# An LSTM with a sign-weight FFN on one core: first x loaded in rows and turned by TensorE, last block's third layer with activations stationary

## The chip, the cores and the metric

One NeuronCore of a Trainium2 chip runs the whole program in one launch. The metric is the device time of one execution in microseconds (us); the median of several runs is compared. The engines are TensorE (PE in the profile, its weight loads PEld), VectorE (DVE), ScalarE (ACT), GpSimd (POOL) and SyncE (SP); SP, ACT and POOL issue DMAs.

## The reference

x is [32, 64, 256], cond is [32, 256]; all floats are float32.

```
xW = einsum('ntd,dg->ntg', x, Wx) + b                # 64 steps, 1024 gate columns
for t in range(64):                                   # LSTM, h0 = cond, c0 = 0
    a = xW[:, t] + h @ Wh
    i, f, o = sigmoid of a's first three quarters;  g = tanh of its last
    c = f * c + i * g;  h = o * tanh(c);  hs[:, t] = h
v = concatenate([hs, -hs], axis=-1)                   # [32, 64, 512]
v = relu(s0 * (v @ pm1(k0))) * 2                      # 1024 features
v = relu(s1 * (v @ pm1(k1))) * 2                      # 1024 features
out = x + s2 * (v @ pm1(k2))                          # 256 features
```

`pm1(k)` is +1 where the boolean is true, else -1. The scales s0, s1, s2 are scalars.

## The kernel before, in words

The 32 batch rows are N, the 64 steps are T. The steps form four blocks of 16 (SB), each block two halves of eight steps. The hidden width of 256 is cut into four quarters of 64 (NQ, HQ); quarter q lies on partitions 32q to 32q+31, so a step's gates fill 128 partitions.

Loading. `load_x` (L88 to L96) brings one half of a block's x with four DMAs, one for each quarter: 32 partitions, eight steps, runs of 64 floats (256 B). `turn_x` (L226 to L231) turns it with VectorE's transpose of 32x32 blocks into `xT`, which holds x with the input dimension on partitions. `load_gates` (L118 to L129) loads column groups ("slots") of Wx or Wh; the gate order in the tile is (3, 0, 1, 2). Wx's rows are taken in two chunks k, since the input dimension 256 is 128 partitions by two. At the start (L132 to L141) SP and ACT issue in this order: x of the first half, Wx's chunks, x of the second half, Wh. GpSimd issues `h_first` (cond, L145), the bias rows and the scales, and then computes the signs and `total`, the product of scales used at the end.

The completion marks of SP's and ACT's DMAs are eight in number and are shared in turn, in the order of issue; a DMA that reuses a mark waits until the earlier DMA has landed.

The start of TensorE (L640 to L643) is two matmuls that fill the gate banks with zeros and eight idle ones (`WARM_UP`), all from a zeroed bf16 tile `idle` of 128x512. Then come the products of x with Wx for the first eight steps: chunk 0, slots 1 and 2, then slots 0 and 3 (L669 to L671, through `x_part` L242); the bias broadcast by matmuls (`copy_bias`, L654); chunk 1 with all slots (L673), each pair of steps evicted by VectorE with the bias added (`evict_x`).

The steps. For each of the 64 steps `gates_from_h` (L301) adds h times Wh to gates that ScalarE has set from the x products, `cell_step` (L319) does the nonlinear part on ScalarE and VectorE, and h is turned into the history. Behind each step's gates TensorE is given a share of other work, by a goal written out by hand: first the remaining x products, then the FFN of the blocks that are complete. FFN operands are split in a high and a low part (fp32r), so each product takes two matmuls.

The last block (`last_block`, L417) has nothing beside it. Its second layer is computed by sums and differences of quarters; its third layer is at L550 to L583. There `layer2` holds a 128x128 piece of `w2` stationary and streams 256 columns of activations; the result has output features on partitions, two banks for each half of the block (eight steps by 32 rows). `turn_out` (L384) turns a result with VectorE into the layout of x, `scale_out` (L387) multiplies by `total` and adds x, and `store` (L377) writes it with four DMAs of 64 KB in runs of 256 B, alternating SP and ACT. The residual x of the block is loaded again by `load_x` at L497.

Of the kernel before, what the change touches and what calls it, by code (L numbers as in the profile page):

```python
# [29 lines left out]
F32 = mybir.dt.float32  # L33
# [3 lines left out]
ALU = mybir.AluOpType  # L37
# [4 lines left out]
def lstm_ffn(ctx: ExitStack, tc: tile.TileContext, x, cond, wx_d, wh_d, b_d, k0_d, k1_d, k2_d, s0_d, s1_d, s2_d, out):  # L42
    nc = tc.nc
    P = 128
    N, T, D = x.shape
    H = cond.shape[1]
    G = 4 * H
    NQ = 4
    HQ = H // NQ
    F0 = k0_d.shape[1]  # L50
    F1 = k1_d.shape[1]
    FC0, FC1 = F0 // P, F1 // P
    SB = 16
    NB = T // SB
    TB = SB * N
    SH = 4
# [5 lines left out]

    FIRST_CHORE = 2
    W2_STEP = 24
    WARM_UP = 8

    SUM_STEP = 28

    const = ctx.enter_context(tc.tile_pool(name="const", bufs=1))
    wpool = ctx.enter_context(tc.tile_pool(name="wx", bufs=1))  # L70
    xpool = ctx.enter_context(tc.tile_pool(name="x", bufs=4))
# [6 lines left out]
    ps_f = ctx.enter_context(tc.tile_pool(name="ps_f", bufs=4, space=PSUM))  # L78
    ps_o = ctx.enter_context(tc.tile_pool(name="ps_o", bufs=2, space=PSUM))
    ctx.enter_context(tc.manual_schedule())  # L80

    def act(shape, dtype, name):
        return apool.tile(shape, dtype, tag="act", name=name)


    xq = {}

    def load_x(i, half, engines, part=slice(0, SB // 2)):  # L88
        if part.start == 0:
            xq[i, half] = xpool.tile([P, SB // 2, HQ], F32, tag="x", name=f"x{i}_{half}")  # L90
        t0 = i * SB + half * (SB // 2)
        for q in range(NQ):
            engines[q % len(engines)].dma_start(
                out=xq[i, half][q * N : (q + 1) * N, part],
                in_=x[:, t0 + part.start : t0 + part.stop, ts(q, HQ)],
            )  # L96
# [5 lines left out]
    wx = wpool.tile([P, 2, G], F32, tag="wx", name="wx")  # L102
    w0 = const.tile([P, 2, F0], F32R, name="w0")
    w1 = const.tile([P, FC0, F1], F32R, name="w1")
    w2 = const.tile([P, 2, FC1, P], F32R, name="w2")

    warm = const.tile([P, 40], F32, name="warm")
    nc.vector.memset(warm, 0.0)
    idle = const.tile([P, 512], mybir.dt.bfloat16, name="idle")
    nc.vector.memset(idle, 0.0)  # L110

    first = warm[:, 4 : 4 + N]
    nc.vector.memset(first[:1], 1.0)
# [4 lines left out]
    def load_gates(t, w_d, slots, engines, chunks=slice(0, 2)):  # L118

        w_rows = w_d.rearrange("(p b) g -> p b g", b=2)  # L120
        s0, n, g0 = slots[0], len(slots), GATES[slots[0]]
        if len(engines) == 1:
            halves = [slice(0, P)]
        else:
            halves = [slice(0, P // 2), slice(P // 2, P)]
        for engine, half in zip(engines, halves):
            engine.dma_start(
                out=t[half, chunks, s0 * H : (s0 + n) * H], in_=w_rows[half, chunks, g0 * H : (g0 + n) * H]
            )  # L129


    both = [nc.sync, nc.scalar]  # L132
    load_x(0, 0, both)
    for k in range(2):
        load_gates(wx, wx_d, (1, 2), [nc.sync], slice(k, k + 1))
        for slot in (0, 3):
            load_gates(wx, wx_d, (slot,), [nc.scalar], slice(k, k + 1))
    load_x(0, 1, both)
    load_gates(wh, wh_d, (1, 2), both)
    load_gates(wh, wh_d, (0,), [nc.scalar])  # L140
    load_gates(wh, wh_d, (3,), [nc.sync])  # L141

    nc.scalar.activation(warm[:, 1:2], warm[:, :1], AF.Sigmoid)
    h_first = const.tile([P, HQ], F32, name="h_first")
    nc.gpsimd.dma_start(out=h_first, in_=cond.rearrange("n (q j) -> q n j", q=NQ))  # L145
    b_rows = b_d.rearrange("(o g h) -> o g h", o=1, g=4)
    nc.gpsimd.dma_start(out=b_row[0][:1, :1], in_=b_rows[:, 3:])
    nc.gpsimd.dma_start(out=b_row[0][:1, 1:], in_=b_rows[:, :1])
    nc.gpsimd.dma_start(out=b_row[1][:1], in_=b_rows[:, 1:3])
    scales = []  # L150
    for i, s_d in enumerate((s0_d, s1_d, s2_d)):
        s = const.tile([P, 1], F32, name=f"s{i}")
# [7 lines left out]
    for i in range(2):  # L160
        t = act([P, 2, F0], U8, f"k0_{i}")
# [17 lines left out]
    total = const.tile([P, 1], F32, name="total")  # L179
# [44 lines left out]
    xT = {}  # L224

    def turn_x(i, half, part=slice(0, SB // 2)):  # L226
        if part.start == 0:
            xT[i, half] = act([P, SB // 2, 2, N], F32, f"xT{i}_{half}")
        nc.vector.transpose(
            xT[i, half][:, part], xq[i, half][:, part].rearrange("p t (j b) -> p t b j", b=2)  # L230
        )  # L231
# [10 lines left out]
    def x_part(p, t, k, slots, start):  # L242

        i, s = divmod(t, SB // 2)
        for q in range(NQ):
            nc.tensor.matmul(  # L246
                p[q * N : (q + 1) * N, t % 2, slots],
                xT[i // 2, i % 2][:, s, k, :],
                wx_q[:, k, q, slots],
                start=start,  # L250
                stop=False,
                skip_group_check=True,
            )
# [123 lines left out]
    def store(b, half, o, engines):  # L377
        t0 = b * SB + half * (SB // 2)
        for q in range(NQ):
            engines[q % len(engines)].dma_start(  # L380
                out=out[:, t0 : t0 + SB // 2, ts(q, HQ)], in_=o[q * N : (q + 1) * N]
            )

    def turn_out(o, p, m):  # L384
        nc.vector.transpose(o[:, :, m, :], p.rearrange("p (t n) -> p t n", n=N))

    def scale_out(o, res):  # L387
        nc.vector.scalar_tensor_tensor(o, o, total, res, ALU.mult, ALU.add)  # L388


    K2, F2, CB = FC0 // 2, F1 // 2, TB // 2
# [25 lines left out]
    def last_block(b):  # L417

        hi, lo = hparts.pop(b)
        full, b11, b2, t, a1 = [], {}, {}, {}, {}  # L420
# [55 lines left out]
        for m in range(FC0):  # L476
            p = ps_f.tile([P, TB], F32, tag="pf", name=f"p0_{b}_{m}")
# [5 lines left out]
            if m < K2:  # L483
# [3 lines left out]
                f = f[:, 0]  # L487
# [6 lines left out]
                    differ(i, m - K2 - 1)  # L494
            yield

        for half in range(2):  # L497
            load_x(b, half, [nc.sync])
        for i in (1, 2):
            differ(i, K2 - 1)  # L500

# [42 lines left out]
        for pair in range(2):  # L544
            product(q, pair, lambda k: sums[4, k], lambda k, n: b2[k][n][:, 1], False, True)
            take(0, 1, pair, q[pair])

        po = [ps_o.tile([P, TB], F32, tag="po", name=f"po{b}_{m}") for m in range(2)]  # L550
        po_half = {
            (0, 0): po[0][:, :CB],
            (0, 1): po[0][:, CB:],
            (1, 0): po[1][:, :CB],
            (1, 1): ps_f.tile([P, TB], F32, tag="pf", name=f"po{b}_2")[:, :CB],
        }

        def layer2(half, m, ks, first, last):
            for k in ks:
                for n in range(2):  # L560
                    nc.tensor.matmul(  # L561
                        po_half[half, m],
                        w2[:, m, k],
                        a1[k, half][n],
                        start=first and k == ks[0] and n == 0 and (half, m) != (0, 1),
                        stop=last and k == ks[-1] and n == 1,
                        skip_group_check=True,
                    )

        os = [act([P, SB // 2, 2, 32], F32, f"o{b}_{half}") for half in range(2)]  # L570
        for ks in (range(K2), range(K2, FC0)):
            for m in range(2):
                layer2(0, m, ks, ks[0] == 0, ks[0] > 0)
        for m in range(2):
            turn_out(os[0], po_half[0, m], m)
        o = os[0].rearrange("p t m j -> p t (m j)")
        scale_out(o, xq[b, 0])
        store(b, 0, o, [nc.sync, nc.scalar])
        for m in range(2):
            layer2(1, m, [*range(K2, FC0), *range(K2)], True, True)  # L580
            turn_out(os[1], po_half[1, m], m)
            scale_out(os[1][:, :, m, :], xq[b, 1][:, :, ts(m, 32)])
        store(b, 1, os[1].rearrange("p t m j -> p t (m j)"), [nc.sync, nc.scalar])  # L583

    def ffn_block(b):
        hi, lo = hparts.pop(b)
# [50 lines left out]
    outputs = deque()  # L637

    p_idle = ps_f.tile([P, TB], F32, tag="pf", name="p_idle")
    for g in gate_banks:  # L640
        nc.tensor.matmul(g, idle[:, :P], idle, start=True, stop=True)  # L641
    for n in range(WARM_UP):
        nc.tensor.matmul(p_idle, idle[:, :P], idle, start=True, stop=True)  # L643
    turn_x(0, 0, slice(0, SB // 4))
    turn_x(0, 0, slice(SB // 4, SB // 2))
    for i in range(4):
        load_bits(i)
    for half in range(2):
# [5 lines left out]
    def copy_bias():  # L654
        p_bias = ps_o.tile([P, 4, HQ], F32, tag="po", name="p_bias")
        for q in range(NQ):
            for i, t in enumerate(b_row):
                nc.tensor.matmul(  # L658
                    p_bias[q * N : (q + 1) * N, 2 * i : 2 * i + 2],
                    first,  # L660
                    t.rearrange("p g (q j) -> p q g j", q=NQ)[:, q],
                    start=(i == 0),
                    stop=True,
                    skip_group_check=True,
                )
        nc.vector.tensor_copy(bias, p_bias)

    banks = [x_bank(t) for t in range(0, SB // 2, 2)]
    for slots in (slice(1, 3), slice(0, 4, 3)):  # L669
        for t in range(SB // 2):  # L670
            x_part(banks[t // 2], t, 0, slots, t % 2 == 0 and slots.start == 1)  # L671
    copy_bias()
    for t in range(SB // 2):  # L673
        x_part(banks[t // 2], t, 1, slice(0, 4), False)
        if t % 2:
            evict_x(banks[t // 2], t - 1)
            if t == 1:
                turn_x(0, 1)
# [89 lines left out]
```

## Time and profile before

| what | value |
|---|---|
| median of 3 runs | 312.65 us (312.47 to 313.43) |
| the profiled execution's own time | 312.31 us |
| its span | 310.5 us |
| mean granted TensorE clock | 0.998 |
| TensorE busy | 304.5 us, 98% of the span |
| VectorE, ScalarE, GpSimd busy | 178.1, 142.0, 6.6 us |

The span is the time from the first to the last event that the profile holds; some 1.8 us lie around it. Busy time counts instructions of an engine, not its waiting for others. The chain of waits is followed back from the last instruction: at each step to what released it. In the list of instructions a line number is that of the kernel, and "x64" means that so many instructions in a row are merged.

### The profile page before, as it was taken

What the parts mean: (1) busy time and instruction counts of PE and PEld (TensorE: products, weight loads), DVE (VectorE), ACT (ScalarE), POOL (GpSimd) and SP (SyncE); (2) the same over time, 40 slices, a digit from 0 to 9 for tenths busy, and PEclk for the clock granted to TensorE, in tenths of its full rate; (3) what the DMA queues carried; (4) which work ended last, traced back from release to release, by engine and by line L of the source; (5) the groups of instructions that cost most, each with busy time, mean ns of one, the idle gap of its engine ahead of it and who ended that gap; (6) DMA issues with size and microseconds to landing.
All of it is one profiled execution on the core that took longest, in us unless ns stands there. A gap on an engine that the chain in (4) does not pass through costs nothing.

```text
span 310.5 us, 9798 instructions
## 1 busy us (share of the span) xinstructions
PE 304.5 (98%) x4138; PEld 242.7 (78%) x4138; DVE 178.1 (57%) x530; ACT 142.0 (46%) x512; POOL 6.6 (2%) x24
## 2 busy tenths in 40 slices
PE   8999999999999999999999999999999999999994
PEld 4888888788777777777777777777777777899993
DVE  2566767777673444355754445567554434698543
ACT  0225566774564543435633434355443333886220
POOL 5300000000000000000000000000000000000000
PEclk9999999999999999999999999999999999999999
DMA  6874001142000000000010000000310000131002
GB/s 192 206 196 99 5 19 38 36 95 65 3 2 0 2 2 0 3 2 0 2 38 22 14 3 0 2 2 13 92 34 2 3 0 2 31 79 27 2 0 69
DMA packets 30587, 10.89 MB, mean 35 GB/s; under 512 B 27720, under 2 KB 29768, under 8 KB 30544
## 3 DMA queue, kind: packets, MB, share of 16 engines
q1 hardware_dynamic: 27136, 8.66, 11.2%
q10 hardware_dynamic: 3168, 1.57, 2.0%
q8 instruction: 32, 0.52, 0.7%
q0 software_dynamic: 240, 0.04, 0.1%
q14 instruction: 11, 0.09, 0.1%
HBM read 8.16 MB, written 2.10 MB: 33 GB/s over the span
## 4 chain that ended last, share of the span: by engine, by line
PE 97%; DVE 1%; ACT 0%; issue 0%; ACTq 0%
PE p L617 30%; PE gates L305 20%; PE px L246 18%; PE p L591 8%; PE po L604 7%; PE gates L452 4%; PE po L561 2%; PE r L452 2%; PE x L452 2%; PE p L479 2%; PE p_idle L643 1%; PE gates L641 0%; DVE a_7l L362 0%; DVE o L388 0%; PE p_bias L658 0%
## 5 line engine op out<-in xcount | busy, mean ns | idle before, releaser
L305 PEld LDWEIGHTS gates<-wh,hist 128*32 128x32 f32 x2016 | 54.6, 109 | 22.3 <-issue 13.4
L305 PE MATMUL gates<-wh,hist 128*32 128x192 f32 x2016 | 68.1, 275 | 0.0
L246 PE MATMUL px<-wx,xT 128*32 128x256 f32 (+1 forms) x1168 | 60.5, 353 | 0.1
L322 ACT ACTIVATE sig<-gates 128x128 f32<-128x128 f32 x64 | 17.7, 277 | 80.6 <-PE gates L305 80.4
L246 PEld LDWEIGHTS px<-wx,xT 128*32 128x32 f32 x1168 | 42.4, 110 | 11.3 <-DVE c_first L652 0.7
L326 DVE TENSOR_TENSOR kept<-sig,c 128x64 f32<-128x64 f32 x63 | 14.2, 225 | 50.0 <-ACT sig L322 49.7
L332 ACT ACTIVATE th<-c 128x64 f32<-128x64 f32 x64 | 16.4, 257 | 31.4 <-DVE c L330 31.4
L334 DVE TENSOR_TENSOR h<-sig,th 128x64 f32<-128x64 f32 x64 | 14.4, 225 | 20.7 <-ACT th L332 20.7
L262 DVE TENSOR_TENSOR xg<-px,bias 128x512 f32<-128x512 f32 x32 | 21.2, 671 | 2.8 <-PE px L246 2.3
L316 ACT COPY gates<-xg 128x192 f32<-128x192 f32 x64 | 20.0, 313 | 1.3 <-DVE xg L262 1.3
L591 PE MATMUL p<-hhi,w 128*128 128x512 f32 x48 | 19.3, 402 | 0.0
L591 PE MATMUL p<-hlo,w 128*128 128x512 f32 x48 | 19.1, 398 | 0.0
L339 DVE STREAM_TRANSPOSE hist<-h 128x64 f32<-128x64 f32 x64 | 15.7, 245 | 2.4
L330 DVE TENSOR_TENSOR c<-kept,new 128x64 f32<-128x64 f32 x64 | 14.4, 224 | 2.2
L324 ACT ACTIVATE sig<-gates 128x64 f32<-128x64 f32 x64 | 14.9, 233 | 0.1
L323 ACT ACTIVATE cand<-gates 128x64 f32<-128x64 f32 x64 | 14.0, 218 | 0.0
L328 DVE TENSOR_TENSOR new<-sig,cand 128x64 f32<-128x64 f32 x64 | 13.9, 217 | 0.0
L317 ACT COPY gates<-xg 128x64 f32<-128x64 f32 x64 | 13.0, 203 | 0.0
L591 PEld LDWEIGHTS p<-hhi,w 128*128 128x128 f32 x48 | 9.0, 188 | 2.2
L591 PEld LDWEIGHTS p<-hlo,w 128*128 128x128 f32 x48 | 9.0, 188 | 2.0
L211 ACT ACTIVATE w<-bits,nsgn,sgn 128x1024 fp32r<-128x1024 uint8 x8 | 9.9, 1241 | 0.0
L617 PE MATMUL p<-a_7h,w 128*128 128x512 f32 x24 | 9.9, 413 | 0.0
(249 smaller groups left out, 602.8 us busy)
## 6 DMA issues: line engine op xcount, KB each, us to landing
x<-in_x_dram SPq DMA_DIRECT2D x60, 64.0 KB, 2.8
out_dram<-o SPq DMA_DIRECT2D x28, 64.0 KB, 1.8
bits<-in_L_ffn_k_dram SPq DMA_DIRECT2D x10, 128.0 KB, 3.2
wx<-in_L_cond_Wx_dram SPq DMA_DIRECT2D x2, 256.0 KB, 4.2
wx<-in_L_cond_Wx_dram ACTq DMA_DIRECT2D x4, 128.0 KB, 4.6
wh<-in_L_cond_Wh_dram ACTq DMA_DIRECT2D x2, 256.0 KB, 5.6
wh<-in_L_cond_Wh_dram SPq DMA_DIRECT2D x2, 256.0 KB, 6.2
k<-in_L_ffn_k_dram SPq DMA_DIRECT2D x2, 256.0 KB, 3.1
```

Of the source, the lines that this page charges most:

```text
L246: nc.tensor.matmul(p[q * N : (q + 1) * N, t % 2, slots], xT[i // 2, i % 2][:, s, k, :], wx_q[:, k, q, slots], start=start, stop=False, ski ...
L262: nc.vector.tensor_tensor(xg[t], p.rearrange("p t g j -> p t (g j)"), b, ALU.add)
L305: nc.tensor.matmul(g[q * N : (q + 1) * N], hT[:, k, :], wh_q[:, k, q, slots], start=False, stop=(k == 1), skip_group_check=True,)
L316: nc.scalar.copy(gates[0], x_t[:, :3])
L322: nc.scalar.activation(sig[:, 0:2, :], gates[0][:, 1:3], AF.Sigmoid)
L324: nc.scalar.activation(sig[:, 2, :], gates[1][:, 0], AF.Sigmoid)
L332: nc.scalar.activation(th, c, AF.Tanh)
L339: nc.vector.transpose(hT, h.rearrange("p (j b) -> p b j", b=2))
L452: nc.tensor.matmul(bank[pair][:, i], a(k)[:, ts(2 * pair + i, P)], b(k, n), start=first and i == 0 and k == 0 and n == 0, stop=last and k ...
L591: nc.tensor.matmul(p, w0[:, k, ts(m, P)], a[:, k, :], start=(n == 0), stop=(n == 3))
L604: nc.tensor.matmul(po[m], w2[:, m, k], a1[k][n], start=(k == 0 and n == 0), stop=(k == FC1 - 1 and n == 1))
L617: nc.tensor.matmul(p1[m], w1[:, k, ts(m, P)], a0[k][n], start=(k == 0 and n == 0), stop=(k == FC0 - 1 and n == 1),)
```

## The change

Four things are changed.

- The first half of block 0 is loaded as rows: a partition is one (step, batch row) pair and holds the 256 inputs, 1 KB. Steps 0 to 3 come in two DMAs (SP and ACT, two steps each), steps 4 to 7 in one (ACT). TensorE turns them against an identity in float32, VectorE copies the result to `xT`. GpSimd makes the identity (a memset and an `affine_select`) ahead of its DMAs, and `h_first` moves behind the bias rows.
- Wx's pieces are issued in another order and cut, and the products follow it: chunk 0 of steps 0 to 3 in both pairs of slots, then steps 4 to 7. The bias matmuls move behind the second step of chunk 1.
- The warm-up is three idle matmuls ahead of the first turn and two behind it (eight before), from a bf16 tile of 128x128 that is read four times over.
- In the last block, the third layer holds 128 columns of activations stationary (four steps by 32 rows) and streams a row of `w2`, 256 columns. The result has (step, batch row) on partitions, so it is scaled and added to x from PSUM in one instruction and stored unturned: two DMAs of 64 KB for each four steps, one on SP and one on ACT, in runs of 1 KB. The residual x is loaded in the same layout, four DMAs of 128 KB on SP.

```diff
-    WARM_UP = 8
+    WARM_UP = (3, 2)
...
+    x_in = x
+    def rows_of(t, t0, n):
+        return t[:, t0 : t0 + n].rearrange("n t d -> t n d")
...
+    idle = const.tile([P, P], mybir.dt.bfloat16, name="idle")
+    nc.vector.memset(idle, 0.0)
     nc.vector.memset(warm, 0.0)
-    idle = const.tile([P, 512], mybir.dt.bfloat16, name="idle")
-    nc.vector.memset(idle, 0.0)
...
+    ident = act([P, P], F32, "ident")
+    nc.gpsimd.memset(ident, 1.0)
+    nc.gpsimd.affine_select(
+        out=ident, in_=ident, pattern=[[-1, P]], compare_op=ALU.is_equal, fill=0.0, base=0, channel_multiplier=1
+    )
     both = [nc.sync, nc.scalar]
-    load_x(0, 0, both)
-    for k in range(2):
-        load_gates(wx, wx_d, (1, 2), [nc.sync], slice(k, k + 1))
-        for slot in (0, 3):
-            load_gates(wx, wx_d, (slot,), [nc.scalar], slice(k, k + 1))
+    x_first = xpool.tile([P, 2, D], F32, tag="x", name="x_first")
+    for s, engine in enumerate(both):
+        engine.dma_start(out=x_first[ts(s, P // 2), 0], in_=rows_of(x_in, s * SH // 2, SH // 2))
+    load_gates(wx, wx_d, (1, 2), both, slice(0, 1))
+    nc.scalar.dma_start(out=x_first[:, 1], in_=rows_of(x_in, SH, SH))
+    load_gates(wx, wx_d, (3,), [nc.sync], slice(0, 1))
+    load_gates(wx, wx_d, (0,), [nc.scalar], slice(0, 1))
+    load_gates(wx, wx_d, (1, 2, 3), [nc.sync], slice(1, 2))
+    load_gates(wx, wx_d, (0,), [nc.scalar], slice(1, 2))
     load_x(0, 1, both)
...
-        for half in range(2):
-            load_x(b, half, [nc.sync])
+        res = [xpool.tile([P, 2, D], F32, tag="x", name=f"res{half}") for half in range(2)]
+        for i in range(NQ):
+            nc.sync.dma_start(out=res[i // 2][:, i % 2], in_=rows_of(x_in, b * SB + i * SH, SH))
...
+        po = [ps_o.tile([P, TB], F32, tag="po", name=f"po{b}_{i}") for i in range(2)]
+        po += [ps_f.tile([P, TB], F32, tag="pf", name=f"po{b}_{2 + i}") for i in range(2)]
+        def layer2(i, ks):
+            half, cols = i // 2, ts(i % 2, P)
             for k in ks:
                 for n in range(2):
                     nc.tensor.matmul(
-                        po_half[half, m],
-                        w2[:, m, k],
-                        a1[k, half][n],
...
+                        po[i][:, :D].rearrange("p (q m j) -> p q m j", q=NQ, m=2),
+                        a1[k, half][n][:, cols],
+                        w2[:, :, k].rearrange("p m (q j) -> p q m j", q=NQ),
+                        start=k == order[half][0] and n == 0,
+                        stop=k == order[half][-1] and n == 1,
                     )
+        def finish(i):
+            o = act([P, D], F32, f"o{b}_{i}")
+            nc.vector.scalar_tensor_tensor(o, po[i][:, :D], total, res[i // 2][:, i % 2], ALU.mult, ALU.add)
+            for s, engine in enumerate((nc.sync, nc.scalar)):
+                t0, n = b * SB + i * SH, SH // 2
+                engine.dma_start(out=rows_of(out, t0 + s * n, n), in_=o[ts(s, P // 2)])
+        order = [[*range(FC0)], [*range(K2, FC0), *range(K2)]]
         for ks in (range(K2), range(K2, FC0)):
-            for m in range(2):
-                layer2(0, m, ks, ks[0] == 0, ks[0] > 0)
...
+            for i in range(2):
+                layer2(i, ks)
+        for i in range(2):
+            finish(i)
+        for i in range(2, 4):
+            layer2(i, order[1])
+            finish(i)
...
+    def turn_first(i):
+        p = ps_o.tile([P, 2, SH, N], F32, tag="po", name=f"px_first{i}")
+        for k in range(2):
+            nc.tensor.transpose(p[:, k].rearrange("p t n -> p (t n)"), x_first[:, i, k::2], ident)
+        for k in range(2):
+            nc.vector.tensor_copy(xT[0, 0][:, ts(i, SH), k, :], p[:, k])
...
-    for n in range(WARM_UP):
-        nc.tensor.matmul(p_idle, idle[:, :P], idle, start=True, stop=True)
-    turn_x(0, 0, slice(0, SB // 4))
-    turn_x(0, 0, slice(SB // 4, SB // 2))
+        nc.tensor.matmul(g, idle, zeros, start=True, stop=True)
+    warm_up(WARM_UP[0])
+    turn_first(0)
+    warm_up(WARM_UP[1])
...
-    for slots in (slice(1, 3), slice(0, 4, 3)):
-        for t in range(SB // 2):
-            x_part(banks[t // 2], t, 0, slots, t % 2 == 0 and slots.start == 1)
-    copy_bias()
+    for i in range(2):
+        for slots in (slice(1, 3), slice(0, 4, 3)):
+            for t in range(i * SH, (i + 1) * SH):
+                x_part(banks[t // 2], t, 0, slots, t % 2 == 0 and slots.start == 1)
+            if i == 0 and slots.start == 1:
+                turn_first(1)
     for t in range(SB // 2):
         x_part(banks[t // 2], t, 1, slice(0, 4), False)
+        if t == 1:
+            copy_bias()
```

## The prediction

> **What bounds the kernel now.** I read the page first, for the engine that fills the span and for the chain that ends last.
>
> ```profile
> span 310.5 us, 9798 instructions
> PE 304.5 (98%) x4138; PEld 242.7 (78%) x4138; DVE 178.1 (57%) x530; ACT 142.0 (46%) x512; POOL 6.6 (2%) x24
> PE 97%; DVE 1%; ACT 0%; issue 0%; ACTq 0%
> ```
>
> TensorE works 304.5 of 310.5 us. What it does not fill is about 1.2 us before its first instruction and 4.5 us after its last, so an edit counts only if it moves TensorE's first useful product, lengthens TensorE's stream, or moves what follows the last matmul. A shift at the start passes to the end nearly one to one. Next the chain of waits at both ends (start, duration, what):
>
> ```profile
> 2.27 3.23 PE p_idle L643 x8
> 5.51 1.89 PE px L246 x64
> ...
> 298.26 7.69 PE po L561 x64
> 305.95 0.02 issue
> 305.98 0.46 DVE o L385
> 306.43 0.03 issue
> 306.46 0.48 DVE o L388
> ```
>
> Useful products begin at 5.51, when the idle warm-up matmuls end; x was ready just before (the timeline has the two turns of x on VectorE from 4.32 for 0.77, to 5.09). After the last matmul come a turn, a scaling and a store: 306.94 to 310.5. The DMA view of 306.9 to 309.2 shows the last store's bytes from 307.76 to 309.08, so 0.8 us from result to first byte, 1.3 us of bytes, 1.45 us from last byte to the end of the span.
>
> Then what a DMA engine moves, from the windows table (length, five engines' busy time, clock, DMA share of 16 engines, GB/s):
>
> ```profile
> 18.00:19.00 1.00, 1.00 (x25) 0.85 (x21) 0.64 (x4) 0.55 (x4) 0.00 (x0) 1.00 1.02 352
> 308.50:309.00 0.50, 0.00 (x0) 0.00 (x0) 0.00 (x0) 0.00 (x0) 0.00 (x0) 0.98 1.08 245
> ```
>
> Loads of 2 and 1 KB rows: 352 / 1.02 / 16 = 21.6 GB/s per engine. Stores of 256 B rows: 245 / 1.08 / 16 = 14.2 GB/s per engine.
>
> Last, how transfers are spread. Every transfer of SP and ACT in before has 32 or more steps as the outermost count of both sides. The change makes transfers whose DRAM side is (t, n, d) with t outermost: 2 steps for the first x pieces and all eight last stores, 4 for the second x piece and the residual loads. One transfer of before resembles them: `h_first` (L145), 4 outermost steps in DRAM against 128 partitions, issued by GpSimd.
>
> ```profile
> DMA packets 30587, 10.89 MB, mean 35 GB/s; under 512 B 27720, under 2 KB 29768, under 8 KB 30544
> ```
>
> Between 2 and 8 KB lie 30544 - 29768 = 776 packets. The 2 KB rows of Wx (256), Wh (256) and k0 (256) make 768; the other 8 are `h_first`, 32 KB in packets of 4,096 B, each 16 rows of 256 B. Sixteen engines would have had 8 rows each, 2,048 B. So at most eight engines carried it: a transfer with few outermost steps was not spread over all. That row decides my forecast.
>
> **The change, part by part.**
>
> *Third layer.* 64 matmuls of 128x256 before and after, with 64 loads of 128 columns, 0.12 us apart. Only which operand stands still is exchanged, and 256 columns stream either way: no change. A tile of four steps is now complete as rows, and the first ends with the 24th matmul: 298.10 + 23 x 0.12 + 0.28 = 301.1.
>
> *Tail on VectorE.* The turn (0.46 + 0.03) goes. Each tile takes one scaling of 256 columns, 0.48 by L388. The first tile is ready at 301.7, the last at 306.46 instead of 306.94.
>
> *Stores.* Bytes start 0.8 us after a tile, at 302.5. In all 524,288 B leave. On two engines that is 262,144 B each, at 21.6 GB/s 12.1 us. The tiles come 0.9 to 2 us apart and each needs 3.0 us, so there is no gap: 302.5 + 12.1 + 1.45 = 316.1, **5.5 us later** than 310.5. Bounds with two engines: 25 GB/s, the fastest 0.1 us slice of the opening (401 GB/s over 16), gives 10.5 us and +3.9; 14.2 GB/s gives 18.5 us and +11.9. I take 21.6, because the new rows are 1 KB. On sixteen engines the last 131,072 B take 0.6 us: 306.46 + 0.8 + 0.6 + 1.45 = 309.3, 1.2 us earlier.
>
> The Trainium skill (DMA: Bandwidth & Descriptors, "Why a DMA increments its semaphore by 16 and not by 1") says that a transfer uses the largest number of engines up to 16 that divides the outermost count of both sides, the lowest-numbered ones. `h_first` agrees, on another queue and without giving the exact number; by the rule the tail is +5.5, by the spread of before's own stores it is -1.2.
>
> *First x.* SP and ACT issue at 0.73 as before, first bytes at 1.7. On two engines 65,536 B each at 21.6 GB/s take 3.0 us; with about 0.5 for the completion mark x stands at 5.2, where 16 engines give about 2.9. TensorE now needs two f32 transposes and a copy of 128 columns on VectorE. Neither has a row: a transpose lies between 0.12 (a 256-column matmul here) and 0.43 (a slow warm-up), I take 0.3; the copy lies between 0.23 (64 columns) and 0.42 (256), I take 0.3. Two warm-ups of 0.43 stand behind the transposes in TensorE's order: 5.2 + 0.6 + 0.86 gives 6.7, by VectorE alone 6.1; 6.4, **+1.0** against 5.44. The three warm-ups fewer give nothing, since they now end before x.
>
> *Order of pieces.* Rows of x for steps 4 to 7 (128 KB, four engines) queue on ACT behind Wx's first piece. The lowest engine holds 64 + 16 + 8 + 32 KB and part of Wx's next rows, 120 to 144 KB, at 21.6 GB/s 5.7 to 6.8 us: marks at 7.9 to 9.0, say 8.5. TensorE reaches the second transposes at 6.4 + 0.98 (32 instructions of 30 ns) = 7.4, waits **1.1**, transposes **0.6**, then waits **0.3** for slot 0, behind x on the same queue. Start: **+3.0**. Lower bound +1.0 if the second x is on time; upper +5: before's warm-ups run at 0.43 us for 512 columns until at least 4.6, the po matmuls at 0.24, and a pause from 3.2 to 5.2 may begin that slow stretch anew, up to 1.7 us.
>
> *Lanes of completion.* Eight marks are shared by the transfers of SP and ACT in turn, so Wx's last piece and x's second half wait for the first x pieces. Wh then lands near 14, for a need at 16.4 + 3. ACT's table load stands behind its issues (8.73 before), about 10 now, for a need at 11.6 + 3. Covered: nothing.
>
> *GpSimd.* The identity is made ahead of the bias loads, and the one library load in the program moves ahead of it, from L169. There it lies in the idle 3.10 us from 5.29 to 8.38, so it costs 0 to 3.1; the identity is ready by 4.4, under x at 5.2. Bias loads shift to about 4.4 + 1.5 and land near 10.5, for a need near 13; with x early, that load would be what the transposes wait for. The residual loads (128 KB on four engines, 6 us, issued near 275) end long before 301.
>
> The Trainium skill (GPSIMD Engine Reference, "Instruction dispatch") gives about 6 us for the first call to a freshly loaded kernel; the row above leaves no room for that. By the page the identity would come at 7.3 and the start would cost about +3.8.
>
> *Sum.* The profiled execution took 312.31 us for a span of 310.5; 312.31 + 5.5 + 3.0 = **320.8**. The median of the runs, 312.65, is 0.3 above it.
>
> **The rivals.** *All sixteen engines carry each transfer* (the other side). Place: the spread of the 2-step pieces; price: tail -1.2; start: x at 2.9, the five warm-ups end near 3.2 (first one near 1.0, since the idle tile is smaller), products at 3.2 + 0.6 + 0.86 = 4.7, 0.8 early, less the second transposes' 0.6: -0.2; with the library load at 3.1 the first transposes begin at 4.4 and it is +1.0. 310.9 to 312.1; I take 310.9, as no row shows any load time. For it: SP and ACT may split by the 64 partitions of the on-chip side. Against it: `h_first` has 128 there and was not spread. It decides from about eight engines on, where the last 131,072 B take under 1 us. *Only the stores are narrow* (split by destination): 312.31 + 5.5 - 0.2 = 317.6. *Only the loads are narrow* (split by source): 312.31 + 3.0 - 1.2 = 314.1. Against both: in `h_first` the source was the 4-step side and the destination the 128-partition side, which excludes splitting by destination alone; nothing excludes the second. *The change's shorter tail is hidden anyway*: no, nothing stands behind it.
>
> **How the numbers follow.** Two engines, both ends: 0.83, at 320.8, own range 317.3 (1.0 + 3.9) to 329 (5 + 11.9). Sixteen: 0.10. Stores only: 0.02. Loads only: 0.05. Leaving out sixteen, the loads-only case and the slowest stores, the range is 316.0 to 325.5. About 0.3% (0.9 us) is what a measurement can tell from no change. Faster 0.09 and same 0.03, the ends of the sixteen-engine case and a little of the loads-only one; slower 0.88.
>
> **What would show it.** Right: the last store bytes run at about 43 GB/s with a DMA share near 0.13 for some 12 us, from before the last matmul to about 5 us past the old end; TensorE idle between its third warm-up and about 5.2, and once more before the second transposes. Wrong: stores near 200 GB/s, or the transposes waiting for GpSimd, or po matmuls not 0.12 apart.

## The result and the profile after

| | before | after |
|---|---|---|
| median of the runs | 312.62 us (4 runs, 312.47 to 313.43) | 326.12 us (4 runs, 325.32 to 326.28) |
| ratio, 95% interval | | 1.0423 (1.0404 to 1.0442) |
| span of the profiled execution | 310.5 us | 324.3 us (its own time 326.05) |

The changed kernel is 13.5 us slower, 0.6 us above the upper end of the range. First the head of its page, and its DMA line:

```profile
span 324.3 us, 9800 instructions
PE 307.3 (95%) x4139; PEld 244.0 (75%) x4139; DVE 176.7 (54%) x529; ACT 142.0 (44%) x512; POOL 7.1 (2%) x26
DMA packets 26338, 10.88 MB, mean 34 GB/s; under 512 B 22320, under 2 KB 25520, under 8 KB 26296
```

TensorE's share falls from 98 to 95%: it stands still for 17.0 us where it stood for 6.0. It also works 2.8 us longer. The chain of waits shows where the idle time lies (start, duration, what):

```profile
2.53 9.17 DMA x_first<-in_x_dram
12.44 5.50 PE px L266 x112
...
305.87 7.63 PE po L577 x64
313.50 0.03 issue
313.53 0.48 DVE o L587
```

The head of the chain was TensorE; now it is a transfer of x, 128 KB that take 9.17 us. The third layer begins at 305.87 in place of 298.26 (**+7.6**) and takes 7.63 in place of 7.69. From its end to the end of the span it was 4.55 us and is 10.8 (**+6.25**). These two make the 13.8 us between the spans. TensorE's timeline resolves the first of them:

```profile
1.86 1.49 PE L661 MATMUL p_idle<-idle 128*128 128x512 bf16 x3
7.37 0.67 PE L666 MATMUL px_first<-ident,x_first 128*128 128x128 f32 x2 [4.03 <-DMA x_first<-in_x_dram]
7.83 1.06 PE L661 MATMUL p_idle<-idle 128*128 128x512 bf16 x2
8.82 1.94 PE L266 MATMUL px<-wx,xT 128*32 128x128 f32 x32
11.74 0.70 PE L666 MATMUL px_first<-ident,x_first 128*128 128x128 f32 x2 [0.98 <-DMA x_first<-in_x_dram]
12.37 5.57 PE L266 MATMUL px<-wx,xT 128*32 128x128 f32 x112
```

Two waits for x, 4.03 and 0.98 us. Between them 32 products take 1.94 us, 60 ns each, where the kernel before did 128 in 4.03 us, 31 ns each:

```profile
5.44 4.03 PE L246 MATMUL px<-wx,xT 128*32 128x128 f32 x128
```

The windows table of the changed kernel shows the end (length, five engines' busy time, clock, DMA share of 16 engines, GB/s):

```profile
314.00:318.00 4.00, 0.00 (x0) 0.00 (x0) 0.01 (x1) 0.00 (x0) 0.00 (x0) 0.83 0.14 47
320.00:322.00 2.00, 0.00 (x0) 0.00 (x0) 0.00 (x0) 0.00 (x0) 0.00 (x0) 0.50 0.14 48
```

No engine works, and the stores run at 47 to 48 GB/s with 0.14 of sixteen DMA engines, that is about two. The first store byte moves at 310.5, the last at 323.05.

### The profile page after: what moved, and what is told of

Read it like the earlier page. It is cut to its first block, busy times and chain, and to the rows that moved or that the text cites. A ratio compares the mean times of both kernels' runs of the same rounds, so it can differ in the third digit from the quotient of the medians.

```text
span 324.3 us, 9800 instructions
## 1 busy us (share of the span) xinstructions
PE 307.3 (95%) x4139; PEld 244.0 (75%) x4139; DVE 176.7 (54%) x529; ACT 142.0 (44%) x512; POOL 7.1 (2%) x26
## 4 chain that ended last, share of the span: by engine, by line
PE 92%; DMA 3%; DVE 1%; ACTq 1%; ACT 0%; issue 0%
PE p L634 29%; PE gates L325 19%; PE px L266 17%; PE p L608 7%; PE po L621 7%; PE gates L472 4%; DMA x_first<-in_x_dram 3%; PE r L472 2%; PE x L472 2%; PE po L577 2%; PE p L499 2%; ACTq L151 0%; PE px_first L666 0%; DVE a_7l L382 0%; ACTq L136 0%; PE p_bias L688 0%
## 5 line engine op out<-in xcount | busy, mean ns | idle before, releaser
L266 PE MATMUL px<-wx,xT 128*32 128x256 f32 (+1 forms) x1168 | 63.1, 366 | 0.0
L266 PEld LDWEIGHTS px<-wx,xT 128*32 128x32 f32 x1168 | 43.5, 116 | 12.6 <-DVE c_first L682 0.8
```

Of the source, the lines that this page charges most:

```text
L266: nc.tensor.matmul(p[q * N : (q + 1) * N, t % 2, slots], xT[i // 2, i % 2][:, s, k, :], wx_q[:, k, q, slots], start=start, stop=False, ski ...
```

## The experiments

In the table, "start" is by how much later than in the kernel before the last `po` matmul ends (305.94 there), and "end" is from there to the end of the span (4.56 there), both from each kernel's profiled execution. The ratio is to runs of the kernel before on the same chip.

| kernel | median us | ratio, 95% interval | start | end |
|---|---|---|---|---|
| the changed kernel | 326.12 | 1.0423 (1.0404 to 1.0442) | +7.5 | 10.8 |
| stores_by_step | 317.78 | 1.0168 (1.0133 to 1.0203) | +5.3 | 3.85 |
| x_by_step | 324.29 | 1.0355 (1.0311 to 1.0400) | +2.9 | 11.0 |
| both_by_step | 316.65 | 1.0107 (1.0059 to 1.0154) | +5.0 | 4.0 |
| idle_matmuls_in_waits | 323.80 | 1.0366 (1.0343 to 1.0390) | +4.9 | 11.3 |
| both_wx_cut_as_before | 314.59 | 1.0050 (1.0024 to 1.0076) | +1.7 | 3.9 |
| both_h_first_first | 315.25 | 1.0080 (1.0061 to 1.0099) | +3.2 | 4.0 |
| before_last_block_by_step | 311.73 | 0.9969 (0.9950 to 0.9987) | +0.2 | 3.8 |
| before_last_block_narrow | 319.27 | 1.0213 (1.0193 to 1.0232) | 0.0 | 11.5 |
| four_steps | 318.04 | 1.0173 (1.0156 to 1.0190) | +5.3 | 5.0 |
| x_by_sequence_stores_by_step | 313.20 | 1.0026 (1.0002 to 1.0051) | +0.7 | 3.8 |
| x_by_sequence_wx_cut | 312.45 | 1.0006 (0.9984 to 1.0028) | +2.5 | 3.75 |
| x_by_sequence_wx_cut_h_first | 313.49 | 1.0034 (1.0012 to 1.0056) | +1.4 | 3.7 |

The end repeats from kernel to kernel. The start does not: both_by_step ran from 313.62 to 316.89, x_by_sequence_stores_by_step from 312.14 to 315.96 in ten runs, where 25 runs of the kernel before lay within 312.15 to 313.27. For starts the median counts, and a single profile only shows what can happen: the profiled execution of x_by_step took 321.56 us (its other three 324.15 to 324.78), that of both_wx_cut_as_before 313.23, that of x_by_sequence_stores_by_step 312.19, that of x_by_sequence_wx_cut 313.94, so their rows under "start" lie 2.7, 1.4 and 1.0 us below and 1.5 above what their medians would give.

### Are the stores narrow because of their two steps?

stores_by_step cuts each tile's store into one transfer for each step:

```diff
-            for s, engine in enumerate((nc.sync, nc.scalar)):
-                t0, n = b * SB + i * SH, SH // 2
-                engine.dma_start(out=rows_of(out, t0 + s * n, n), in_=o[ts(s, P // 2)])
+            for s in range(SH):
+                engine = (nc.sync, nc.scalar)[s % 2]
+                engine.dma_start(out=out[:, b * SB + i * SH + s], in_=o[ts(s, N)])
```

> Only the last stores differ from the changed kernel: each tile leaves in four DMAs of 32 KB, one for each step, whose outermost count is 32 batch rows on both sides, still in rows of 1 KB. Theory N (a transfer of two outermost steps runs on two DMA engines): the time from the last matmul to the end of the span falls from 10.8 us to about 4, bytes leave at over 150 GB/s, 326.1 - 6.9 = about 319.2 us. Rival W (stores in rows of 1 KB, or from this layout, are slow in themselves): still about 43 GB/s and 326 us.

317.78 us. The end falls from 10.8 to 3.85 us with the same bytes in the same 1 KB rows and twice the transfers; only the outermost count went from 2 to 32. The DMA view of the last 25 us of the changed kernel (40 equal slices, GB/s):

```profile
GB/s 0 0 0 0 0 0 0 0 0 0 0 0 0 0 0 0 5 18 39 25 33 33 46 43 48 49 48 49 48 48 49 48 48 49 48 48 21 0 0 13
```

and the same of the last 15 us of stores_by_step:

```profile
GB/s 0 0 0 0 0 0 0 0 0 0 0 0 0 0 0 0 0 0 0 0 40 138 165 151 130 68 0 0 148 132 65 0 0 151 127 68 0 0 0 0
```

One flat stretch at 48 becomes three short bursts of up to 165 GB/s, one for the first two tiles and one each for the third and the fourth.

four_steps moves one transfer of four steps for each tile, and for the first piece of x:

```diff
-            for s, engine in enumerate((nc.sync, nc.scalar)):
-                t0, n = b * SB + i * SH, SH // 2
-                engine.dma_start(out=rows_of(out, t0 + s * n, n), in_=o[ts(s, P // 2)])
+            engine = (nc.sync, nc.scalar)[i % 2]
+            engine.dma_start(out=rows_of(out, b * SB + i * SH, SH), in_=o)
...
-    for s, engine in enumerate(both):
-        engine.dma_start(out=x_first[ts(s, P // 2), 0], in_=rows_of(x_in, s * SH // 2, SH // 2))
+    nc.sync.dma_start(out=x_first[:, 0], in_=rows_of(x_in, 0, SH))
```

> The changed kernel with each store, and the first piece of x, as one transfer of four steps in place of two transfers of two steps: as many bytes, half as many transfers. Theory N (the number of engines that carry a transfer is the number of its outermost steps, at about 24 GB/s each): four engines move 96 GB/s, the last tile's 131,072 B take 1.4 us, the end from the last matmul falls from 10.8 to about 4.5 us; the first x is on the chip at about 4.5 in place of 7.3 and TensorE's first transposes start then; the median comes to about 317. Rival W (what is slow is the 1 KB rows or the two queues sharing them, whatever the steps): the end stays at 10 us or more, the first transposes at 7, and the median at 325 or more.

318.04 us; the end is 5.0 us (expected 4.5), the first transposes begin at 5.41 (expected about 4.5). Its windows table between the last tile's first and last bytes:

```profile
313.50:314.50 1.00, 0.00 (x0) 0.00 (x0) 0.00 (x0) 0.00 (x0) 0.00 (x0) 0.77 0.27 97
```

97 GB/s with 0.27 of sixteen engines: about four of them. Two steps 48, four steps 97: the rate goes with the count of outermost steps, not with the queues (a tile left on two at once there, on one here) nor with the rows (1 KB in both).

### Do the two parts add up?

Both kernels are the one before with only its last block exchanged: before_last_block_narrow takes it exactly as changed, before_last_block_by_step stores it by step, as stores_by_step does, and loads its residual by step too:

```diff
-            nc.sync.dma_start(out=res[i // 2][:, i % 2], in_=rows_of(x_in, b * SB + i * SH, SH))
+            for s in range(SH):
+                nc.sync.dma_start(out=res[i // 2][ts(s, N), i % 2], in_=x_in[:, b * SB + i * SH + s])
```

> The kernel before, start untouched, with the last block exactly as changed (stores of two 64-row halves, each on two engines). Theory N: the end grows from 4.55 to 10.8 us as in the changed kernel and nothing else, so 312.6 + 6.25 = about 318.9; the start's share of the whole is then 326.1 - 318.9 = 7.2. Rival R (the tail is longer in the changed kernel because the narrow residual rows or the late start push it): 317.5 or less here.

> The kernel before, start untouched, with the new third layer, and with the residual rows and the stores moved as one transfer for each of the 32-row steps, so that all sixteen engines carry them. Theory N (the two parts of the change are independent, and the third layer's new form costs nothing by itself): the end from the last matmul to the span's end goes from 4.55 us to the 3.8 us seen with the stores by step, so 312.6 - 0.8 = about 311.9, faster than both kernels. Rival R (the unturned third layer or its residual rows cost time somewhere in the middle, which the late start has covered so far): 313 or more.

319.27 and 311.73 us (expected 318.9 and 311.9). So the last block alone costs 6.6 us, and the start the remaining 326.12 - 319.27 = 6.85. The unturned third layer itself costs nothing: its matmuls fill TensorE as before, and with wide stores its end is 0.75 us shorter. before_last_block_by_step beats both kernels, by 0.3% against the one before (interval 0.13 to 0.5%). Its end in VectorE's timeline:

```profile
304.26 0.48 DVE L573 SCALAR_TENSOR_TENSOR o<-po,total,res 128x256 f32<-128x256 f32 x1 [1.42 <-PE po L563]
306.17 0.48 DVE L573 SCALAR_TENSOR_TENSOR o<-po,total,res 128x256 f32<-128x256 f32 x1 [1.42 <-PE po L563]
```

The last scaling ends at 306.65, the span 3.25 us later.

### What does the start lose?

x_by_step loads the first x as eight transfers of one step, alternating between SP and ACT:

```diff
-    for s, engine in enumerate(both):
-        engine.dma_start(out=x_first[ts(s, P // 2), 0], in_=rows_of(x_in, s * SH // 2, SH // 2))
+    for s in range(SH):
+        both[s % 2].dma_start(out=x_first[ts(s, N), 0], in_=x_in[:, s])
...
-    nc.scalar.dma_start(out=x_first[:, 1], in_=rows_of(x_in, SH, SH))
+    for s in range(SH):
+        both[s % 2].dma_start(out=x_first[ts(s, N), 1], in_=x_in[:, SH + s])
```

> Only the first x loads differ from the changed kernel: steps 0 to 7 come in eight DMAs of 32 KB, one for each step, alternating SP and ACT, 32 batch rows as outermost count. Theory N: x stands at about 3.2 us instead of 7.3, the second x is no longer waited for, TensorE's products begin near 5; the start is within 0.5 us of the kernel before, 326.1 - 7.3 = about 318.8 us. Rival T (the turn by TensorE and its slow pace set the start, not the loads): at least 2.6 us of the 7.6 stay, 321.1 us or more.

324.29 us, a miss, and in the range of rival T. Yet x is there as theory N has it: first transposes at 3.50 in place of 7.37, products at 5.16 in place of 8.82. The slow pace has a part (the first 32 products take 1.76 us), and then TensorE waits for something else. both_by_step joins it with the wide stores and residual loads:

> First x loads, residual loads and last stores all by step, 32 batch rows outermost; everything else as in the changed kernel. Theory N: both losses go, 326.1 - 6.9 - 7.3 = about 311.9 us, 0.7 under the kernel before, since the turn on VectorE and half of the last bytes are saved. If W or T holds for part of it, 315 us or more.

316.65 us, 4.7 above the expectation, for the same reason. Its waits of TensorE in the first 20 us (total, times, longest):

```profile
PE px L267 <- DMA wx<-in_L_cond_Wx_dram: 2.5, 1, 2.5
```

The wait that x held up to now passes to Wx's second chunk, 384 KB in rows of 3 KB on SP's queue, which lands 7.6 us after its issue. Theory N was right on x and blind to what is late next.

idle_matmuls_in_waits leaves the loads alone and fills TensorE's two waits:

```diff
-    warm_up(WARM_UP[0])
+    warm_up(14)
     turn_first(0)
...
             if i == 0 and slots.start == 1:
+                warm_up(8)
                 turn_first(1)
```

> The changed kernel with 14 instead of 3 idle matmuls ahead of the first transposes and 8 new ones ahead of the second, so that TensorE works through both waits for x; loads and stores as narrow as in the changed kernel. Theory C (2.6 us of the 7.6 lost at the start are TensorE's slow pace after its pauses): products run at 30 ns an instruction from the first, about 2.6 us are saved there, of which the fixed landing of the second x at 11.7 takes back about 1: about 324.5 us. Rival: the slow pace has another cause (the transposes, the f32 form): 326 us or a little more.

323.80 us, as theory C has it. Two lines of its timeline against those of the changed kernel:

```profile
8.29 1.08 PE L266 MATMUL px<-wx,xT 128*32 128x128 f32 x32 [0.58 <-DVE c_first L682]
11.58 3.69 PE L266 MATMUL px<-wx,xT 128*32 128x128 f32 x112
```

The same 32 products take 1.08 us, not 1.94, and the 112 behind them 3.69, not 5.57. So part of the start was neither a wait nor work: TensorE ran at about half its pace, and work in the waits removes that. It is worth 1.9 us on the 112; what the 32 gain passes into the time until the second x is there. The medians differ by 2.3 us (326.12 - 323.80). In the two profiles the second transposes also begin 0.7 us earlier (11.05 in place of 11.74) and the end is 0.5 us longer (11.3 in place of 10.8), so the 2.3 is not the pace alone. The windows table of the changed kernel shows the change of pace inside the 112 products:

```profile
12.00:16.00 4.00, 4.00 (x70) 3.41 (x73) 0.49 (x2) 0.79 (x2) 1.54 (x9) 1.00 0.89 235
16.00:18.00 2.00, 2.00 (x60) 1.59 (x53) 0.00 (x0) 0.00 (x0) 0.00 (x0) 1.00 0.55 115
```

70 matmuls in 4 us are 57 ns each, 60 in 2 us are 33, and the granted clock in the seventh column says 1.00 in both. When the quick pace returns is not the same in every kernel: stores_by_step has the same start and the same two waits (3.80 and 1.15), yet its 112 took 3.69:

```profile
11.57 0.50 PE L666 MATMUL px_first<-ident,x_first 128*128 128x128 f32 x2 [1.15 <-DMA x_first<-in_x_dram]
12.00 3.69 PE L266 MATMUL px<-wx,xT 128*32 128x128 f32 x112
```

That is the most of the 2.2 us by which its start is shorter in the table. Nor does the slow pace need a long pause: in x_by_step, both_by_step and x_by_sequence_stores_by_step, where the first transposes come at 3.5 and no wait up to the end of the first 32 products exceeds 0.2 us, those 32 still took 1.76, 1.70 and 1.85 us. There TensorE had not yet reached its quick pace; whether the 1.94 here come from the pause of 4.03 us or from that opening is not shown.

### What holds Wx's second chunk?

Three theories: its cut into a 3 KB piece (P); GpSimd's loads, whose eight packets of 4,096 B now fall into its time (G); the five extra transfers of x at the head of the two queues (I). both_wx_cut_as_before and both_h_first_first each change one thing in both_by_step:

```diff
-    load_gates(wx, wx_d, (1, 2, 3), [nc.sync], slice(1, 2))
-    load_gates(wx, wx_d, (0,), [nc.scalar], slice(1, 2))
+    load_gates(wx, wx_d, (1, 2), [nc.sync], slice(1, 2))
+    for slot in (0, 3):
+        load_gates(wx, wx_d, (slot,), [nc.scalar], slice(1, 2))
```

> The kernel with first x, residual and stores moved step by step, with one more edit: Wx's second chunk is cut and queued as in the kernel before (slots 1 and 2 as 2 KB rows on SP, slots 0 and 3 as 1 KB rows on ScalarE's queue) in place of 3 KB rows on SP for slots 1 to 3. Theory P (the 384 KB piece on one queue is what TensorE waits 2.5 us for at its second chunk): the wait falls below 0.5 us and the median comes to about 314. Rival G (what is late there is not the cut: GpSimd's loads of bias rows and h_first, or the number of transfers in flight, hold the DMA engines at that time): the wait stays at 2 us or more and the median at about 316.6.

> The kernel with first x, residual and stores moved step by step, with one more edit: GpSimd issues h_first ahead of the three bias rows, as in the kernel before. Theory P (the cut of Wx's second chunk causes the wait): nothing changes, the wait for Wx stays at about 2.5 us and the median at about 316.6. Rival G (h_first's eight packets of 4,096 B, which now fall into the time of that piece, hold the engines): the wait falls to about 1 us or less and the median comes to about 314.5.

314.59 and 315.25 us, 2.1 and 1.4 below the 316.65 they started from, and in both profiles waits for Wx of 1.6 us in all remain. Each theory said that one of the two would change nothing, and neither did; with the spread of this start the pair decides little.

x_by_sequence_stores_by_step removes the extra transfers of x; residual and stores stay by step. It puts x on the partitions in the order (sequence, step), so that the outermost count of each piece is 16 or 32 with no transfer more than in the changed kernel; the copies undo the order:

```diff
-        engine.dma_start(out=x_first[ts(s, P // 2), 0], in_=rows_of(x_in, s * SH // 2, SH // 2))
+        engine.dma_start(out=x_first[ts(s, P // 2), 0], in_=x_in[ts(s, N // 2), :SH])
...
-    nc.scalar.dma_start(out=x_first[:, 1], in_=rows_of(x_in, SH, SH))
+    nc.scalar.dma_start(out=x_first[:, 1], in_=x_in[:, SH : 2 * SH])
...
-            nc.vector.tensor_copy(xT[0, 0][:, ts(i, SH), k, :], p[:, k])
+            nc.vector.tensor_copy(xT[0, 0][:, ts(i, SH), k, :], p[:, k].rearrange("p n t -> p t n"))
```

> The changed kernel with the first x in the order sequence, step on the partitions (the copies behind the transposes undo the order), so that its three transfers have 16 and 32 outermost rows and go over all sixteen engines without a transfer more, and with residual and stores step by step. Theory I (in the versions with x step by step, the five extra x transfers at the head of the two queues pushed Wx's second chunk back): first transposes at about 3.5, the wait for Wx's second chunk under 1 us, and the median at about 313.5. Rival P (the 3 KB piece itself is late, whatever stands ahead of it): the wait stays at 2 us and the median at 315.5 or more.

313.20 us, as theory I has it (313.5), though one of the ten executions took 315.96. The timeline of TensorE in an execution of 312.19:

```profile
3.49 0.67 PE L667 MATMUL px_first<-ident,x_first 128*128 128x128 f32 x2
3.96 1.06 PE L662 MATMUL p_idle<-idle 128*128 128x512 bf16 x2
5.17 1.85 PE L266 MATMUL px<-wx,xT 128*32 128x128 f32 x32 [0.15 <-DMA wx<-in_L_cond_Wx_dram]
6.96 0.51 PE L667 MATMUL px_first<-ident,x_first 128*128 128x128 f32 x2
7.39 3.69 PE L266 MATMUL px<-wx,xT 128*32 128x128 f32 x112
```

All waits for transfers together are 0.15 us. x comes in as many transfers and in rows of the same size as in the changed kernel, and Wx in the order of the change; of the start only the outermost count of x and the order of its rows differ. Of the start's 6.85 us remain 313.20 - 311.73 = 1.5 by medians, against the same last block behind the old start.

The last two add Wx's cut of before, and then h_first ahead of the bias rows:

> The kernel before this one in the list (x in sequence order, residual and stores step by step), with Wx's second chunk cut as in the kernel before. Theories I and P together: no wait above 0.5 us is left before the products, and the median comes to about 312.3, within 0.3% of the kernel before; if I alone holds, the same 313.5 as without the cut; if P alone, 314.

> The same again with h_first issued ahead of the bias rows on GpSimd. Theory G (h_first's eight packets of 4,096 B hold engines when Wx's second chunk moves): 0.5 us or more faster than without it. Rival: the same within 0.5 us. With the end worth -0.9 (the kernel before with this last block ran at 311.7) and the start no later than in the kernel before, this is the version of the changed start that could beat the kernel before: 311.7 or less if the changed start is worth anything.

312.45 and 313.49 us. The first is the same as the kernel before within what can be told; from 313.20 its interval overlaps, so P is not shown. With h_first first it is 1.0 slower, not 0.5 faster: on this start G falls (the two intervals overlap, so no more than that is said). None of the versions with the changed start is below 311.73, so the changed start, even with wide loads, has shown no gain. What makes Wx's pieces land early in one execution and late in the next stays open.

## Why the prediction was wrong

The direction and both mechanisms held: transfers with two outermost steps went over two DMA engines, at both ends, and the rivals with sixteen engines at either end fell. The size was off: 13.8 us between the spans, 8.5 forecast. The terms:

- **Spread of the stores.** Right, and the row of `h_first` did point to it. The Trainium skill (DMA: Bandwidth & Descriptors, "Why a DMA increments its semaphore by 16 and not by 1") derives the count of engines from the outermost counts. The shares here agree: 0.14 of sixteen engines for two steps, 0.27 for four.
- **End, +5.5 forecast, +6.25 measured.** The first tile came on time, 4.25 us ahead of the last matmul's end, as forecast. From there to the first byte it took 1.25 us, not 0.8; the bytes 12.55, not 12.1; from the last byte to the end 1.25, not 1.45. The 0.8 was read from a wide store. That the bytes came so near is partly luck: the steady rate was 24 GB/s for each of the two engines, above the 21.6 taken, but the first slices with bytes in the DMA view above show only 18 to 46 GB/s for both together in place of 48.
- **Third layer.** Right: 7.63 us in place of 7.69, and the isolated last block shows no cost.
- **First x, +1.0 forecast, +3.4 measured.** The step that failed is the landing time of x, here and in the next term. I put the mark at 5.2 and it came at 7.3. The rate of a row was not the error: 1 KB took 46 ns, so each piece of 64 rows is 1.5 us on two engines. But ACT's took from 2.2 to 5.3 and SP's from 4.0 to 7.3. Both issues took longer than those of before (1.16 us on ACT, 0.72 on SP, against 0.44), and Wx's 2 KB rows moved at the same time, single ones of them for up to 1.27 us. I charged x's bytes at the engines' full rate from 1.7 on, as if nothing else were on these two engines. The late begin of SP's rows does not explain it: in stores_by_step, with the same loads, rows of both queues moved from 2.3 and 2.5 on, and the first transposes still began at 7.16. What held the two engines below that rate no run separates; that it goes with the two outermost steps x_by_step shows (3.50).
- **Second x.** Wait 1.1 forecast, 0.98 measured, by luck. Its mark was put at 8.5, at most at 9.0, and came at 11.70, and the chain passes through this transfer: the full rate was charged here too. TensorE came as late to it (10.76 in place of 7.4), so the wait looks right. Transposes 0.6, measured 0.63 between the wait and the next product. The wait for slot 0 (0.3) did not come.
- **Pace of TensorE, 0 taken, up to 1.7 as bound.** 0.9 on the 32 products and 1.9 on the 112 behind, 2.8 by these lines; the 0.9 was spent while the second x was still on its way. I had the mechanism, chose the wrong end and set the upper end too low: the slow stretch lasted from 8.8 to about 16, not one warm-up's length. Sum of the start along TensorE: 3.4 + 0.9 + 1.6 + 1.9 = 7.8; by the chain, the forecast 3.0, plus 3.2 for the second x, less 0.3 for slot 0, plus 1.9 of pace, the same 7.8, against 7.6 seen. The Trainium skill (TensorE: Matmul & The Clock Gate, "Part 1: The HAM clock gate") says that a pause of about 3.4 us halves the clock and that about as long a busy time restores it. The pause of 4.03 us here fits, and so does 57 against 33 ns, though the products at 53 to 58 ns in the kernels with an early x had no such pause; the profile's column of the granted clock does not show it. The time back to the quick pace is not settled: some 8.6 us after the pause here, with a wait of 0.98 us in between, under 5 us in stores_by_step.
- **GpSimd.** Right that the identity is not on the path, wrong on the price of the library load: nothing is seen of it. POOL's timeline:

```profile
0.78 0.20 POOL L142 MEMSET ident<- 128x128 f32 x1 [0.29 <-POOLq L790]
1.06 0.29 POOL L143 TENSOR_SCALAR_AFFINE_SELECT ident<-ident 128x128 f32<-128x128 f32 x1
```

The identity stands at 1.35 us, 0.08 us lie between the two instructions, and the 6 us that the page quoted in the prediction names do not appear.

What the sum lacked altogether did not show in the changed kernel but in its repairs: behind a late x stands Wx, so mending x by more transfers gave back only 1.8 us (326.12 to 324.29) of the 7.

## What to carry to other kernels

Write the slowest dimension of a transfer so that its count is 16 or 32 on both sides, as in the wide transfers here; a rearranged view that puts a count of 2 or 4 outermost stored here at 48 or 97 GB/s, in pieces of 64 and 128 KB. If the order is awkward, change the order on the partitions and undo it in a copy that is there anyway, rather than cut the transfer: with five more transfers at the head of the queues, what was queued behind them came 2.5 us too late. Where TensorE must wait at the start, price the pause twice, once as the wait and once as the slow pace that follows, and ask what is late next before counting the repair.

## What the runs showed of the hardware

- Two narrow transfers of 64 KB, issued at 0.78 us on two queues, had their first rows moved at 2.2 (ACT) and 4.0 us (SP) in the changed kernel, at 2.5 and 2.3 in stores_by_step; both times TensorE could use x only after 7.1 us. With the same rows spread over sixteen engines (x_by_step), rows moved from 1.8 on and all 128 were through by 3.0.
- TensorE's pace was halved, 57 against 33 ns, in stretches whose granted clock reads 1.00.
- Of the seven kernels whose first x goes over sixteen engines, five vary by 3.0 to 3.8 us between executions (4 or 10 of each); 25 executions of the kernel before vary by 1.1 us.
